# The last group's layer 2 ends and is normalized by pairs of graphs, and all written-out orders of a four-layer graph network are replaced

## The chip, the cores and the metric

The kernel runs on one core of a Trainium2 chip. The metric is device time in microseconds; lower is better. All arithmetic is fp32. TensorE (PE) does the matmuls, VectorE (DVE), ScalarE (ACT) and GpSimd (POOL) do the rest, and SyncE (SP) issues all DMAs in one queue, in order.

## The reference

`x` holds 128 graphs of 128 nodes with 512 features, `adj` a 128 x 128 matrix for each graph. Four layers follow one another; each output is `x = layernorm(x + layer(x, adj))`. Cut to what matters:

```python
# layer 0: GCN, adjacency with self loops, normalized on both sides
An = dh[:, :, None] * (A + I) * dh[:, None, :]          # dh = rsqrt(row sums)
out = relu(einsum('bnm,bmf,fc->bnc', An, X, kernel) + bias)

# layer 1: attention whose weight is one number for a node
q, k = split(X @ W_qk.T);  v = X @ W_v.T                 # 2 x 64 and 512 columns
w = sum((q @ k.T) / 8 * A, axis=-1);  out = softmax(w, axis=nodes) * v

# layer 2: SAGE, own features beside the neighbours' mean
agg = (A @ X) / max(row sums, 1e-6)
out = relu(concat([X, agg]) @ W.T)

# layer 3: GCN again, projection first, without relu
out = L @ (X @ W + b)                                    # L = normalized A + I
```

The norm has no weights: mean and variance over the 512 features of a node, with 1e-5 added to the variance.

## The kernel before

**Groups.** The 128 graphs are taken in 32 groups `t` = 0 to 31 of four graphs, g = 2q + r. Three groups are in flight: while group t runs layer 0 and then layer 1, group t - 1 runs layers 2 and 3. Group 31 is called `last`; its layers 2 and 3 stand alone at the end, with nothing of another group beside them. Groups 0 and 1 have an order of their own (`begin`), since all weights are loaded and prepared there.

**Products.** The 512-wide projections are blocked twofold with seven products in place of eight, B11, T1, T2, B21, B22, T3, T4. Their operands are sums of blocks: of the left side (`agg0s1`, `agg3s2`, `xT1s4`, `inner` and so on, made by POOL or DVE for each group) and of the weights (made once). The four graphs of a group supply the block rows, so `left_sums` needs graphs 2q and 2q + 1 of a pair q. Layer 0 multiplies `agg0` by `wz_sb` into `p_o0`, layer 1 `xT1` by `wv_sb` into `p_v`, layer 2 `xT2` by `wb_sb`, `wa_sb`, `wc_sb` and `wz_sb` in four passes into `p_2x0` to `p_2x3`, layer 3 `agg3` by `wz_sb` into `p_o3`. One 7-piece tile `wz_sb` thus serves layers 0, 2 and 3; for each of them it is filled again piece by piece from copies in DRAM (`w0d`, `w2d`, `w3d`, 256 KB a piece), and a piece can be fetched once the last product on its old contents has run.

**Turning x.** Layers 1 and 2 need `x` transposed. `turn_x` writes it to DRAM (`xT2s`, one transfer for each graph), reads it back block by block (`xT2y`, four reads for each r), and DVE transposes blocks of 32 (`xT2`). In the first groups and the last one, `turn_on_tensor` lets PE do it.

**The end of layer 2.** After the four passes, `y` (the neighbour half) and `v` (the own half, for every node) are complete. For each graph ACT scales its own half into PSUM (`p_2g`), PE adds `arT` times `y` to it, and DVE adds relu of that to `x` and leaves the row sum in a column of `sm`. `norm_last("o2", ...)` then makes the norm for all four graphs at once: the negated mean `nm` (ACT, tile `last1o`), the four sums of squares (ACT, into the single buffer "row"), on POOL the division by 512, the addition of the epsilon (`dme`), the power -1/2 and the product `nmr` (tiles `last3o`, `last4o`), and for each graph a scaling on ACT, or on DVE where it has been moved. `l3_agg` (for the last group `l3_agg_pair`, one pair after another) multiplies the result by the adjacency (`p_agg`), and `l3_out` follows, in the last group by pairs too. The norms of layer 0 and of the last quarter of layer 3 use `bn_stats` instead.

**What sets the order.** Nothing runs in program order. The kernel records every operation with its predecessors (`Plan`), and `schedule` builds each engine's queue from a list of costs. Three written-out tables steer it. `EARLY` shifts the priority of single operations, and `MOVED` names operations that change engine: ACT's copies and scalings go to DVE, two-operand additions change between DVE and POOL. `TIMES` gives for every operation of groups 3 to 29 a due time within a period (`PERIOD` 73637), and within one engine operations with a due time run strictly by it; so the steady groups repeat one order on each of the five queues ("sy", "ve", "gp", "sc", "te"). A key such as `p_o0:3` is the fourth operation on that engine that writes `p_o0` (the product B21), `w0d:2` the third piece fetched (T2). In `MOVED` and `EARLY` the letter in front is the engine, and a letter a, b, c, y or z behind stands for groups 0, 1, 2, 30 or 31. [...] All recorded operations bear line 890 in the profile.

Of the kernel before, what the change touches and what calls it, by code (L numbers as in the profile page):

```python
# [11 lines left out]
FP = mybir.dt.float32  # L12
AF = mybir.ActivationFunctionType
ALU = mybir.AluOpType
AX = mybir.AxisListType

P = 128
K = 32
Q = P // K
G = 4  # L20
F = 512
# [12 lines left out]
    "g:agg0:0": 52, "g:agg0:0b": 110, "g:agg0:0c": -35, "g:agg0:0y": -5, "g:agg0:0z": -425, "g:agg0s1:0": 31,  # L34
    "g:agg0s1:0b": 134, "g:agg0s1:0c": 107, "g:agg0s1:0y": 132, "g:agg0s1:0z": 84, "g:agg0s2:0": 12,
    "g:agg0s2:0b": -210, "g:agg0s2:0c": 123, "g:agg0s2:0y": -361, "g:agg0s2:0z": -261, "g:agg0s4:0": -71,
    "g:agg0s4:0b": -79, "g:agg0s4:0c": 87, "g:agg0s4:0y": 360, "g:agg0s4:0z": 859, "g:agg30:0z": 623,
    "g:agg30s1:0z": 410, "g:agg30s2:0z": 646, "g:agg30s4:0z": 77, "g:agg31:0z": -329, "g:agg31s1:0z": 410,
    "g:agg31s2:0z": 392, "g:agg31s4:0z": 766, "g:agg3:0": 131, "g:agg3:0a": 333, "g:agg3:0b": -88, "g:agg3:0c": -110,
    "g:agg3:0y": -322, "g:agg3s1:0": 75, "g:agg3s1:0a": 528, "g:agg3s1:0b": -174, "g:agg3s1:0c": -73,  # L40
    "g:agg3s1:0y": -982, "g:agg3s2:0": 6, "g:agg3s2:0a": 24, "g:agg3s2:0b": 233, "g:agg3s2:0c": -16,
    "g:agg3s2:0y": 633, "g:agg3s4:0": 130, "g:agg3s4:0a": -4, "g:agg3s4:0b": 225, "g:agg3s4:0c": -489,
    "g:agg3s4:0y": -118, "g:arT:0": -6, "g:arT:0a": 45, "g:arT:0b": -500, "g:arT:0c": -40, "g:arT:0y": -264,
    "g:arT:0z": -170, "g:arT:1": 52, "g:arT:1a": -19, "g:arT:1b": -120, "g:arT:1c": -597, "g:arT:1y": -412,
    "g:arT:1z": 241, "g:d:0": 24, "g:d:0a": 202, "g:d:0b": 597, "g:d:0c": -98, "g:d:0y": 479, "g:d:0z": 577,
    "g:inner:0": 28, "g:inner:0a": -23, "g:inner:0b": 33, "g:inner:0c": -161, "g:inner:0y": -103, "g:inner:0z": -9,
    "g:inner:1": 32, "g:inner:1a": 163, "g:inner:1b": 49, "g:inner:1c": -147, "g:inner:1y": -81, "g:inner:1z": 158,
    "g:inner:2": 62, "g:inner:2a": 14, "g:inner:2b": 333, "g:inner:2c": 228, "g:inner:2y": -362, "g:inner:2z": -769,
    "g:inners1:0": -21, "g:inners1:0a": 207, "g:inners1:0b": 311, "g:inners1:0c": -84, "g:inners1:0y": 211,
    "g:inners1:0z": 1020, "g:inners1:1": 69, "g:inners1:1a": -28, "g:inners1:1b": -19, "g:inners1:1c": 429,  # L50
    "g:inners1:1y": -160, "g:inners1:1z": 52, "g:inners2:0": 6, "g:inners2:0a": 42, "g:inners2:0b": 316,
    "g:inners2:0c": -125, "g:inners2:0y": 934, "g:inners2:0z": 495, "g:inners2:1": 27, "g:inners2:1a": 22,
    "g:inners2:1b": 597, "g:inners2:1c": -319, "g:inners2:1y": 431, "g:inners2:1z": 201, "g:inners4:0": 15,
    "g:inners4:0a": 206, "g:inners4:0b": -185, "g:inners4:0c": 151, "g:inners4:0y": -376, "g:inners4:0z": -365,
    "g:inners4:1": 4, "g:inners4:1a": 46, "g:inners4:1b": 343, "g:inners4:1c": 17, "g:inners4:1y": 855,
    "g:inners4:1z": 35, "g:last3o2_0:0": -2, "g:last3o2_0:0a": -168, "g:last3o2_0:0b": -312, "g:last3o2_0:0c": 71,
    "g:last3o2_0:0y": -1126, "g:last3o2_0:0z": -8300, "g:last3o2_0:1": -5, "g:last3o2_0:1a": -191,
    "g:last3o2_0:1b": 131, "g:last3o2_0:1c": -27, "g:last3o2_0:1y": -274, "g:last3o2_0:1z": -11, "g:last3o2_0:2": -4,
    "g:last3o2_0:2a": -32, "g:last3o2_0:2b": 253, "g:last3o2_0:2c": 125, "g:last3o2_0:2y": 103,
    "g:last3o2_0:2z": -362, "g:last3o3_0:0": 15, "g:last3o3_0:0a": -230, "g:last3o3_0:0b": -70,  # L60
    "g:last3o3_0:0c": -256, "g:last3o3_0:0y": -437, "g:last3o3_0:0z": -808, "g:last3o3_0:1": 22,
    "g:last3o3_0:1a": 380, "g:last3o3_0:1b": -258, "g:last3o3_0:1c": -80, "g:last3o3_0:1y": 1086,
    "g:last3o3_0:1z": 703, "g:last3o3_0:2z": -4121, "g:last3o3_0:3z": 2795, "g:last3o3_1:0z": -1845,
    "g:last3o3_1:1z": 1419, "g:last4o2_0:0": 6, "g:last4o2_0:0a": -46, "g:last4o2_0:0b": -18, "g:last4o2_0:0c": 320,
    "g:last4o2_0:0y": 1210, "g:last4o2_0:0z": 8290, "g:mean_w3:0w": 2, "g:mean_wv:0w": 265, "g:rs:0": -117,
    "g:rs:0a": -100, "g:rs:0b": -43, "g:rs:0c": 86, "g:rs:0y": -127, "g:rs:0z": 357, "g:rstdo0_0:0": 25,
    "g:rstdo0_0:0a": -173, "g:rstdo0_0:0b": 183, "g:rstdo0_0:0c": -144, "g:rstdo0_0:0y": -134, "g:rstdo0_0:0z": -584,
    "g:rstdo0_0:1": 10, "g:rstdo0_0:1a": 160, "g:rstdo0_0:1b": 126, "g:rstdo0_0:1c": 291, "g:rstdo0_0:1y": 1688,
    "g:rstdo0_0:1z": 572, "g:rstdo0_1:0": 36, "g:rstdo0_1:0a": -417, "g:rstdo0_1:0b": 180, "g:rstdo0_1:0c": 120,
    "g:rstdo0_1:0y": -1819, "g:rstdo0_1:0z": -632, "g:rstdo0_1:1": 28, "g:rstdo0_1:1a": 463, "g:rstdo0_1:1b": 20,  # L70
    "g:rstdo0_1:1c": -257, "g:rstdo0_1:1y": 3996, "g:rstdo0_1:1z": 1836, "g:rstdo3_1:0z": -238, "g:rstdo3_1:1z": 2729,
    "g:v1_0:0": 175, "g:v1_0:0a": -3, "g:v1_0:0b": -122, "g:v1_0:0c": 161, "g:v1_0:0y": 536, "g:v1_0:0z": 159,
    "g:v1_0:1": 53, "g:v1_0:1a": -235, "g:v1_0:1b": -130, "g:v1_0:1c": -458, "g:v1_0:1y": -20, "g:v1_0:1z": -54,
    "g:v1_1:0": 2, "g:v1_1:0a": -127, "g:v1_1:0b": -359, "g:v1_1:0c": 283, "g:v1_1:0y": 352, "g:v1_1:0z": 545,
    "g:v1_1:1": -20, "g:v1_1:1a": 3, "g:v1_1:1b": -110, "g:v1_1:1c": 140, "g:v1_1:1y": 268, "g:v1_1:1z": 73,
    "g:v2_0:0": -25, "g:v2_0:0a": -357, "g:v2_0:0b": -330, "g:v2_0:0c": 69, "g:v2_0:0y": -202, "g:v2_0:0z": 138,
    "g:v2_1:0": -30, "g:v2_1:0a": 50, "g:v2_1:0b": 165, "g:v2_1:0c": -151, "g:v2_1:0y": 1510, "g:v2_1:0z": 553,
    "g:w2y1:0w": -79, "g:wa_sb:0w": -55, "g:wb_sb:0w": 48, "g:wb_sb:1w": -280, "g:wb_sb:2w": -90, "g:wb_sb:3w": -170,
    "g:wc_sb:0w": 73, "g:wc_sb:1w": 11, "g:wc_sb:2w": 88, "g:wc_sb:3w": -88, "g:wc_sb:4w": -224, "g:wc_sb:5w": -90,
    "g:xT1:0": -66, "g:xT1:0a": 56, "g:xT1:0b": 74, "g:xT1:0c": -108, "g:xT1:0y": -179, "g:xT1:0z": 469,  # L80
    "g:xT1s1:0": 17, "g:xT1s1:0a": 259, "g:xT1s1:0b": 113, "g:xT1s1:0c": 400, "g:xT1s1:0y": 2729, "g:xT1s1:0z": 1624,
    "g:xT1s2:0": -8, "g:xT1s2:0a": 40, "g:xT1s2:0b": -109, "g:xT1s2:0c": -136, "g:xT1s2:0y": -182, "g:xT1s2:0z": 378,
    "g:xT1s4:0": 19, "g:xT1s4:0a": 169, "g:xT1s4:0b": 19, "g:xT1s4:0c": 3, "g:xT1s4:0y": 257, "g:xT1s4:0z": 172,
    "g:xT2:0": 25, "g:xT2:0a": -1190, "g:xT2:0b": 137, "g:xT2:0c": 150, "g:xT2:0y": -641, "g:xT2:0z": -64,
    "g:xT2:1": 16, "g:xT2:1a": -52, "g:xT2:1b": 897, "g:xT2:1c": 58, "g:xT2:1y": 446, "g:xT2:1z": 651, "g:xT2:2": -34,
    "g:xT2:2a": 54, "g:xT2:2b": -83, "g:xT2:2c": -165, "g:xT2:2y": -342, "g:xT2:2z": 141, "g:xT2s1:0": -35,
    "g:xT2s1:0a": 70, "g:xT2s1:0b": 46, "g:xT2s1:0c": 37, "g:xT2s1:0y": 387, "g:xT2s1:0z": 406, "g:xT2s1:1": 33,
    "g:xT2s1:1a": 218, "g:xT2s1:1b": -344, "g:xT2s1:1c": -47, "g:xT2s1:1y": -1221, "g:xT2s1:1z": -832,
    "g:xT2s2:0": -40, "g:xT2s2:0a": -588, "g:xT2s2:0b": 149, "g:xT2s2:0c": 18, "g:xT2s2:0y": -308, "g:xT2s2:0z": -283,
    "g:xT2s2:1": 47, "g:xT2s2:1a": -167, "g:xT2s2:1b": -30, "g:xT2s2:1c": 52, "g:xT2s2:1y": 1667, "g:xT2s2:1z": 876,  # L90
    "g:xT2s4:0": -25, "g:xT2s4:0a": 166, "g:xT2s4:0b": 536, "g:xT2s4:0c": 103, "g:xT2s4:0y": -764, "g:xT2s4:0z": -38,
    "g:xT2s4:1": 7, "g:xT2s4:1a": -394, "g:xT2s4:1b": -490, "g:xT2s4:1c": 106, "g:xT2s4:1y": -226, "g:xT2s4:1z": 354,
    "s:agg0:0": -59, "s:agg0:0a": -100, "s:agg0:0b": -22, "s:agg0:0c": 4, "s:agg0:0y": 53, "s:agg0:0z": -429,
    "s:agg0:1": 5, "s:agg0:1a": 213, "s:agg0:1b": -168, "s:agg0:1c": -216, "s:agg0:1y": 347, "s:agg0:1z": -324,
# [847 lines left out]
def kernel(  # L942
# [13 lines left out]
    nc = Plan(tc, estimate)  # L956
    B = x.shape[0]
    NT = B // G
    last = NT - 1
# [5 lines left out]
    sp = Pool(nc, ctx.enter_context(tc.tile_pool(name="sp", bufs=3)), 3)  # L965
# [336 lines left out]
    def norm_last(name, t, rows, pairs):  # L1302
# [6 lines left out]
        if name == "o2":  # L1309
            nc.scalar.mul(nm, st["sm", t][:, 2 * rows[0]:2 * rows[0] + n], -1.0 / F)  # L1310
# [514 lines left out]
```

## Time and profile before

| | us |
|---|---|
| runs, median (lowest, highest) | 2421.62 (2421.4, 2425.13) |
| profiled execution, its own time | 2425.63 |
| its span | 2423.8 |
| PE busy in the span | 2358.1 (97%) |
| DVE, ACT, POOL busy | 1759.7 (73%), 1103.7 (46%), 1269.4 (52%) |
| mean granted clock of PE | 0.995 |
| from one `p_ws` to the next, groups 4 to 28, mean and least | 73.28, 72.48 |

Times in the views count from the start of the span. "Idle before" stands in brackets behind a row of the timeline, with what ended it; a row can hold several instructions of one kind (x2), and the time is then that from the first's start to the last's end. `x24` of `p_agg` are three graphs, since an fp32 matmul counts twice and there are four for each graph. DMA-issuing rows on SP ("SPq") show the issue, not the transfer. The view of waits names, for each engine, who came last, with the sum, the number of times and the longest.

### The profile page before, as it was taken

What the parts mean: (1) busy time and instruction counts of PE and PEld (TensorE: products, weight loads), DVE (VectorE), ACT (ScalarE), POOL (GpSimd) and SP (SyncE); (2) the same over time, 40 slices, a digit from 0 to 9 for tenths busy, and PEclk for the clock granted to TensorE, in tenths of its full rate; (3) what the DMA queues carried; (4) which work ended last, traced back from release to release, by engine and by line L of the source; (5) the groups of instructions that cost most, each with busy time, mean ns of one, the idle gap of its engine ahead of it and who ended that gap; (6) DMA issues with size and microseconds to landing.
All of it is one profiled execution on the core that took longest, in us unless ns stands there. A gap on an engine that the chain in (4) does not pass through costs nothing. (4 is left out here: it accounts for less than half of the span.)

```text
span 2423.8 us, 35397 instructions
## 1 busy us (share of the span) xinstructions
PE 2358.1 (97%) x11244; PEld 1938.4 (80%) x11244; DVE 1759.7 (73%) x3611; ACT 1103.7 (46%) x2480; POOL 1269.4 (52%) x1571
## 2 busy tenths in 40 slices
PE   8989999999999999999999999999999999999997
PEld 6767778888878878788878888888888888888776
DVE  5876777677777767777776777777776777777776
ACT  4444444444444445444444444444444444444444
POOL 4345465445565455565455555455654455654434
PEclk9999999999999999999999999999999999999998
DMA  5455575666666665666666756665756675756532
GB/s 148 160 154 162 139 210 167 182 171 183 174 200 166 181 182 170 190 187 172 178 180 174 196 166 182 173 195 168 200 169 180 171 190 169 202 163 189 155 113 79
DMA packets 492106, 417.36 MB, mean 172 GB/s; under 512 B 151824, under 2 KB 375312, under 8 KB 491664
## 3 DMA queue, kind: packets, MB, share of 16 engines
q1 hardware_dynamic: 491920, 415.09, 60.7%
q8 instruction: 91, 1.49, 0.3%
q14 instruction: 95, 0.78, 0.1%
HBM read 297.27 MB, written 117.70 MB: 171 GB/s over the span
## 5 line engine op out<-in xcount | busy, mean ns | idle before, releaser
L890 PE MATMUL p_o<-wz_sb,agg 128*128 128x256 f32 x2048 | 477.5, 380 | 10.0 <-DMA wz_sb<-w0d 3.9
L890 PEld LDWEIGHTS p_o<-wz_sb,agg 128*128 128x128 f32 x2048 | 383.7, 190 | 70.3 <-DMA wz_sb<-w0d 10.9
L890 PE MATMUL p_v<-wv_sb,xT 128*128 128x320 f32 x1024 | 297.1, 433 | 1.3 <-DVE xT L890 1.1
L890 PEld LDWEIGHTS p_agg<-anT,x 128*128 128x128 f32 x2048 | 251.7, 196 | 22.9 <-DVE x L890 8.8
L890 PE MATMUL p_agg<-anT,x 128*128 128x128 f32 x2048 | 257.7, 281 | 9.6 <-DVE x L890 7.0
L890 PEld LDWEIGHTS p_v<-wv_sb,xT 128*128 128x128 f32 x1024 | 191.6, 190 | 87.5 <-DVE xT L890 8.7
L890 ACT COPY agg<-p_agg 128x512 f32<-128x512 f32 (+1 forms) x221 | 116.2, 527 | 252.4 <-PE p_agg L890 251.8
L890 PE MATMUL p_v<-wv_sb,xT1s 128*128 128x320 f32 x768 | 228.1, 433 | 1.5 <-POOL xT1s L890 1.1
L890 PEld LDWEIGHTS p_v<-wv_sb,xT1s 128*128 128x128 f32 x768 | 145.2, 190 | 69.9 <-issue 15.1
L890 PE MATMUL p_o<-wz_sb,agg0s 128*128 128x256 f32 x768 | 183.9, 383 | 11.1 <-DMA wz_sb<-w0d 7.6
L890 DVE TENSOR_TENSOR y<-p_2x,y 128x512 f32<-128x512 f32 (+1 forms) x256 | 158.9, 621 | 38.7 <-PE p_2x L890 34.2
L890 POOL TENSOR_TENSOR y<-u,y 128x1024 f32<-128x1024 f32 (+1 forms) x89 | 178.9, 2010 | 15.0 <-DVE u L890 6.0
L890 PE MATMUL p_o<-wz_sb,agg3s 128*128 128x256 f32 x744 | 176.1, 380 | 1.3 <-POOL agg3s L890 1.3
L890 ACT COPY f_2x<-p_2x 128x512 f32<-128x512 f32 (+1 forms) x122 | 64.7, 531 | 246.4 <-PE p_2x L890 239.8
L890 PEld LDWEIGHTS p_o<-wz_sb,agg0s 128*128 128x128 f32 x768 | 142.6, 190 | 42.8 <-issue 16.9
L890 ACT COPY p_2x<-p_2x 128x512 f32<-128x512 f32 (+1 forms) x216 | 109.1, 516 | 115.5 <-PE p_2x L890 67.6
L890 PEld LDWEIGHTS p_o<-wz_sb,agg3s 128*128 128x128 f32 x744 | 138.9, 190 | 20.2 <-POOL agg3s L890 2.5
L890 POOL TENSOR_TENSOR agg3s<-agg 128x512 f32<-128x512 f32 x29 | 36.7, 1267 | 204.6 <-ACT agg L890 202.2
L890 DVE TENSOR_TENSOR v<-p_v,f_v 128x320 f32<-128x320 f32 x128 | 57.5, 485 | 115.0 <-PE p_v L890 114.8
L890 POOL TENSOR_TENSOR agg<-agg 128x512 f32<-128x512 f32 (+1 forms) x32 | 39.7, 1240 | 190.1 <-DVE x L890 158.6
L890 PE MATMUL p_2g<-y,arT 128*128 128x512 f32 x256 | 121.6, 595 | 2.9 <-DVE y L890 1.8
L890 ACT COPY p_o<-p_o 128x512 f32<-128x512 f32 (+1 forms) x96 | 54.1, 564 | 148.2 <-PE p_o L890 144.4
(233 smaller groups left out, 5322.7 us busy)
## 6 DMA issues: line engine op xcount, KB each, us to landing
wz_sb<-w2d SPq DMA_DIRECT2D x224, 256.0 KB, 3.5
wz_sb<-w3d SPq DMA_DIRECT2D x224, 256.0 KB, 3.8
wz_sb<-w0d SPq DMA_DIRECT2D x203, 256.0 KB, 4.1
x<-in_x_dram SPq DMA_DIRECT2D x31, 1024.0 KB, 5.8
out_dram<-x SPq DMA_DIRECT2D x31, 1024.0 KB, 5.1
xT1s<-x SPq DMA_DIRECT2D x120, 256.0 KB, 2.8
xT1y<-xT1s SPq DMA_DIRECT2D x240, 128.0 KB, 2.7
xT2s<-x SPq DMA_DIRECT2D x120, 256.0 KB, 2.7
```

Of the source, the lines that this page charges most:

```text
L890: op.ins = getattr(getattr(self.nc, op.engine), method)(*[v.real() if isinstance(v, Ref) else v for v in args], **{k: v.real() if isinstan ...
```

## The change

Two things are changed.

1. In `l2_out` of the last group, the loop over the four `p_2g` goes pair by pair (graphs 0, 1, then 2, 3) in place of r by r, and `norm_last` is called after each pair with that pair alone. `norm_last` now takes the columns of the pair out of `sm` and `dme`. For this group there are thus two negated means, two times two squares, and two chains of four POOL operations on two columns, in place of one chain on four. Other groups call it as before.
2. The tables are replaced. In `EARLY` nearly all shifts differ (2226 entries become 2202). In `MOVED` 74 entries go and 57 come. In `TIMES` the same operations get a new order on all five queues; `PERIOD` and the order of the passes stay.

```diff
-            nc.scalar.mul(nm, st["sm", t][:, 2 * rows[0]:2 * rows[0] + n], -1.0 / F)
+            nc.scalar.mul(nm.rearrange("p (r q) -> p r q", r=2),
+                          st["sm", t].rearrange("p (r q) -> p r q", r=2)[:, :, pairs[0]:pairs[-1] + 1], -1.0 / F)
...
             nc.gpsimd.tensor_tensor(rstd.rearrange("p (r q) -> p r q", r=2), rstd.rearrange("p (r q) -> p r q", r=2),
-                                    st["dme", t].rearrange("p (q r) -> p r q", r=2), ALU.add)
+                                    st["dme", t].rearrange("p (q r) -> p r q", r=2)[:, :, pairs[0]:pairs[-1] + 1], ALU.add)
...
         st["sm", t] = sp.tile([P, 4], FP, tag="sm", name=f"smo2_{t}")
-        for r in range(2):
-            for q in range(2):
+        for i in range(2):
+            for j in range(2):
+                r, q = (j, i) if t == last else (i, j)
                 g = 2 * q + r
...
-            norm_stats("o2", t, r, (0, 1))
+            if t == last:
+                norm_last("o2", t, (0, 1), (i,))
+            else:
+                norm_stats("o2", t, i, (0, 1))
```

Of the tables, the entries that the prediction speaks of (steady groups):

```diff
 TIMES, "sy":
-  "xT2y_0:0": 74313, "xT2s_1:0": 74360, "w0d:2": 1056, "xT2y_0:1": 74753
+  "xT2s_1:0": 72660, "w0d:2": 556, "xT2y_0:1": 74253, "xT2y_0:0": 76813
 TIMES, "te":
-  "p_o0:0": 4975, "p_o3:3": 152272, "p_2x0:0": 79264, "p_o0:3": 7384
+  "p_o3:3": 153372, "p_o0:0": 7175, "p_o0:3": 8084, "p_2x0:0": 81764
 MOVED:
-  "s:agg0:0", "s:f_v_0:0", "s:x:9", "s:y1:0", "g:xT1s4:0"
+  "s:agg0:1", "s:p_o0:1", "s:p_v_0:1", "s:v1:1", "s:x:11"
```

A due time of a group's layers 2 and 3 is counted from the group's own start, so `xT2y_0:0` at 74313 falls 676 behind the next group's zero, beside that group's `w0d:2` at 1056. In group 0 the first operation on `ana` (adding the identity) is on DVE now, while the second (the scaling by `d`) stays on POOL; the three of the four sums of layer 0's `wz_sb` that were on POOL are on DVE, where the fourth has been; and two of the four scalings of its layer-2 norm (x:8 and x:10) are on DVE. In the compiled order of the first groups, group 0's first layer-3 `p_agg` comes ahead of group 1's `p_ws`. In the last group `p_2g` keeps its order 0, 2, 1, 3 on PE; the own half of graph 1 is scaled on DVE, and of the four scalings of the norm only that of graph 0 is on DVE (before, that of graphs 0 and 1).

## The prediction

> **What bounds the kernel now.** The page comes first, for the engine that fills the span:
>
> ```profile
> span 2423.8 us, 35397 instructions
> PE 2358.1 (97%) x11244; PEld 1938.4 (80%) x11244; DVE 1759.7 (73%) x3611; ACT 1103.7 (46%) x2480; POOL 1269.4 (52%) x1571
> ```
>
> TensorE is busy for 2358.1 of 2423.8 us. The change adds and removes no matmul, so only the 65.7 us in which PE does nothing (and the half-clock stretches inside the busy time) can be won. The view of time windows places them, cut at the start of group 4's `p_ws` transpose (372.7), of group 28's (2131.43), and at the end of the last `p_2x` product (2387.24; called E below):
>
> ```profile
> 372.70:2131.43 1758.73, 1744.63 (x8355) 1441.56 (x8353) 1282.26 (x2640) 812.53 (x1825) 956.86 (x1176) 1.00 0.64 180
> 2131.43:2387.24 255.81, 249.88 (x1177) 205.08 (x1175) 192.83 (x385) 114.28 (x252) 123.84 (x159) 1.00 0.54 154
> 2387.24:2423.80 36.56, 22.46 (x97) 17.87 (x96) 18.07 (x39) 14.54 (x31) 9.53 (x18) 0.83 0.17 64
> ```
>
> The columns are the stretch, its length, busy PE, weight load, DVE, ACT, POOL, then the clock and the DMA share. PE idles 14.1 us in 24 steady groups, 5.9 in the last groups and 14.1 in the last 36.56 us (of which some 7 lie behind the last product). The head (0 to 372.7) holds the remaining 31. Next the view of PE's waits over the whole span, for the single large ones:
>
> ```profile
> PE p_agg L890 <- DVE x L890: 7.0, 1, 7.0
> PE p_w L890 <- DVE scr L890: 6.1, 1, 6.1
> PE p_a L890 <- POOL ana L890: 3.4, 1, 3.4
> ```
>
> The first is in the tail, the other two in the head. The same view for the steady stretch alone leaves two kinds:
>
> ```profile
> PE p_o L890 <- DMA wz_sb<-w0d: 8.2, 25, 1.0
> PE p_2x L890 <- DVE xT L890: 3.7, 8, 1.0
> ```
>
> The first is a layer-0 product waiting for its piece of `wz_sb`; the second is the first layer-2 product waiting for the transpose of `x`. From one `p_ws` to the next a group takes 73.28 us in the mean and 72.48 at best, so the steady groups together lose about 0.8 us each.
>
> **The steady groups.** One of the slowest (74.92 us from 885.02 on) shows the chain, first on PE and then on SP's queue:
>
> ```profile
> 901.01 0.70 PE L890 MATMUL p_2x<-wb_sb,xT 128*128 128x256 f32 x2 [0.96 <-DVE xT L890]
> 902.10 1.13 PE L890 MATMUL p_o<-wz_sb,agg 128*128 128x256 f32 x4 [0.39 <-DMA wz_sb<-w0d]
> ```
> ```profile
> 892.65 0.32 SPq L890 DMA_DIRECT2D xT2y<-xT2s  x1
> 893.07 0.38 SPq L890 DMA_DIRECT2D xT2s<-x  x1
> 893.55 0.46 SPq L890 DMA_DIRECT2D wz_sb<-w0d  x1
> ```
>
> SP issues in order. At 892.65 it gets past an `xT2y` read that waits until an earlier `xT2s` write has landed; behind it stand the third `xT2s` write and the T2 piece of w0d, both ready before (piece T2's last reader ended some 1.1 us earlier). The new SP order puts those two ahead of that read. The wait itself only moves to the next `xT2y` read, behind which stand three more reads and piece B21, none of them ready sooner. So T2 can go about 1.0 us earlier and the last `xT2s` write about 1.3. On PE the new order swaps layer 3's B21 product with layer 0's B11. Both take 1.73 us: the reader that frees piece B21 ends 1.73 us sooner, and what lies between the fetch and its use grows from 7.3 to 8.6 us. Last, the first `p_2x` product moves behind layer 0's B21 product, 1.73 us later. DVE works against that: two operations (0.70 and about 0.6) now stand before the transpose that it waits for, leaving 0.4, plus the earlier write.
>
> Counting every PE stall above 60 ns in those 24 groups by the product behind it: T1 5.1 us (23 times, its chain unchanged), first `p_2x` 3.7 (8 times, at most 0.96), B21 3.2 (9 times, at most 0.88), T2 1.2. I take 85% of the last three away: 0.85 x 8.1 = 6.9 us, 0.29 per group, and 7.7 us over the 27 groups that follow this order. Bounds: all of them and half of T1's, 10.7 x 27/24 = 12; or nothing.
>
> What the order tightens: layer 2's last product comes 1.73 us sooner after the product before it (4.32 to 2.59, with 1.10 us of slack before on DVE, whose sum now has to be ready about 0.4 us before PE asks); `p_2x` piece 4 of the first pass 1.73 us sooner, slack 0.2 to 1.4; the first `p_2g` 0.9 us sooner behind POOL's 2.36 us `y` addition, slack 0.3. Expected cost 0.06 us per group, 1.7 in all; bounds 0 and 0.8 per group. Four ACT jobs return from DVE (copies of 0.5 to 0.7 us, a scaling of 0.48) and five others of the same sizes go there, one addition returns to POOL (1.27 there, 0.69 on DVE): engines at 73%, 46% and 54% don't bind in sum. Middle: -7.7 + 1.7 = **-6**.
>
> **The head.** The first `ana` addition stood on POOL (7.64, 1.26 us) ahead of the scaling that `p_a` waits for; it goes to DVE behind the `arT` copy (6.74, 0.69), ends at about 8.1, and POOL's scaling (1.04) ends near 9.1 and not 10.01: -0.9. Three of the four `wz_sb` sums move from POOL (1.27 each) to DVE (0.69 each), where `p_o` T2 waits 1.15 us for them; before it, a new order of the four `p_agg` meets a stall of 0.91. Here a rule of the Trainium skill speaks against the move: in "SBUF — State Buffer", section "Terms", VectorE and GpSimd have a shared port pair which one of them holds for a whole instruction while the other stands still. The trace shows it:
>
> ```profile
> 16.82 0.42 DVE L890 TENSOR_TENSOR agg<-agg 128x256 f32<-128x256 f32 x1 [0.84 <-POOL agg0s L890]
> ```
>
> POOL's addition of this size takes 0.73 us at 16.06 and 17.91, but 0.96 at 16.87, beside this row: 0.23 longer. By the rule the three sums on DVE bar POOL for 2.1 us and nothing is won but 3 x 0.58 = 1.7 us of holding; by the row, which is milder, 1.7 plus some overlap. The stalls they can shorten hold only 1.15 + 0.91, so I take -1.3 (bounds 0, if input DMAs, which saturate until 30 us and stand in a new order, become the limit, and -2.1). At 140.4 to 149.4 the hole of 8.1 us is group 0's layer-2 norm: four squares until 145.69, on which the one "row" buffer makes `scr` wait, four POOL operations until 147.77, four scalings on ACT until 150.7. Two of these go to DVE, and the first `p_agg` no longer stands behind `p_ws`: at about 148.1 and not 149.38, -1.3; the 6.1 us wait stays. Head: **-3.5** (bounds -6 and +2).
>
> **The tail.** The chain that ended last:
>
> ```profile
> 2392.76 0.21 ACT last1o L890
> ...
> 2398.38 0.56 DVE x L890
> 2398.94 0.04 issue
> 2398.98 5.48 PE p_agg L890 x24
> 2404.47 0.86 PE p_o L890 x4
> 2405.33 0.89 PE p_agg L890 x8
> ```
>
> Before: the last of four relu-additions ends at E + 5.5; negated mean 0.21, four squares at 0.85, POOL 0.23 + 0.20 + 1.04 + 0.20 with 0.07 between, scaling 0.56: `p_agg` at E + 11.74. After: PE keeps its order 0, 2, 1, 3, so pair 0 waits for the third `p_2g`; the third relu-addition ended at E + 4.6, and the scale of graph 1 on DVE and an earlier last `y1` addition make it 4.3. Then 0.21 + 2 x 0.85 = 6.2; POOL's power on two columns takes 0.70 (layer 1's norm), so 1.33 + 0.3 of gaps = 7.9; scaling 0.56: `p_agg` at **E + 8.5**. Pair 1: ACT is done with its squares at E + 8.1 (a second negated mean, 0.21, and two squares), POOL at E + 9.7, its two scalings on ACT, behind that of graph 1, at E + 11.2. At half clock 24 matmuls of `p_agg` took 5.48, so graphs 0 and 1 fill 8.5 to 12.2 and graph 3 need not wait. `p_o` therefore starts at 14.0 and not 17.2: **-3.2**; the rest runs without a PE gap in both orders. Bounds 0 (pair 1 late by 4) and -6.
>
> Half clock is the second rule. "TensorE: Matmul & The Clock Gate", section "Why this matters for your kernels", asks for no PE gap above some 3 us, else the clock halves. The rows:
>
> ```profile
> 2395.00:2399.00 4.00, 0.02 (x1) 0.02 (x1) 0.62 (x2) 1.94 (x5) 1.67 (x4) 0.50 0.49 180
> 2399.00:2403.00 4.00, 4.00 (x19) 4.00 (x20) 1.85 (x4) 1.09 (x3) 0.00 (x0) 0.50 0.00 0
> ```
>
> The granted clock fell at 2394.09, 2.1 us into a gap of 7.0, and returned at 2404.33, 5.35 us into the work. Full speed (8 in 0.89) would save 5.48 - 2.67 = 2.8 us. The new gap is about 4 us (E + 4.5 to 8.5). By the rule it still halves the clock, gain -3.2; by a gap that falls across two observation windows it doesn't, -6. I take the rule.
>
> **Sum.** -3.5 - 6 - 3.2 = -12.7, and a tenth of that off for waits that appear behind shortened ones: about **-12**. Made on the profiled execution (2425.63 us: span 2423.8 and 1.8 around it), it would come to 2413.6. That execution is 4.0 above the median of the runs, 2421.62, from which I count: **2409.6**.
>
> **Rivals.** (a) *The ends alone move.* The pieces of w0d share 16 DMA engines that are 64% busy; if their landing times and not SP's order set the stalls, the middle stays: 2421.62 - 6 = 2415.6. For it: the T1 stall, 23 times, has no queue in front of it. Against: the `xT2s` write and T2 visibly stand behind a waiting read. (b) *A new stall per group*, the one with the other sign: layer 2's last product, or the first `p_2g`, asks before DVE or POOL has its sum. Each 0.1 us costs 2.7 us over 27 groups; from 0.45 us on the whole gain of 12 is gone, from 0.63 the kernel is measurably slower; 0.7 gives 2428. For it: slacks of 0.2 to 0.4 us on three products. Against: each lies beside slack of the same size. (c) *The pairs bring nothing*: graph 3's scaling ends so late that PE waits again, 12 - 3 = 9: 2412.6.
>
> **How the numbers follow.** The forecast has 0.50, (a) 0.20, (b) 0.15, (c) 0.15. About 0.2%, 4.8 us, is what a measurement of this kernel tells from no change. The forecast and (c) are nearly all faster, (a) at -6 a little more than half, (b) mostly slower: faster 0.70, same 0.17, slower 0.13. The forecast's own range is 2403 to 2416; with (a), (c) and most of (b), and the lower bounds of head, middle and tail together about -20, it is 2401 to 2426.
>
> **What would show it.** Mean group 73.05 us and no more than 1.5 us of waits `p_2x <- xT` and of B21 together; T1's stall as before. First tail `p_agg` at E + 8.5, and its p_agg x24 still near 5.5. First `p_a` wait near 2.5; the `p_w` wait unchanged. Waits of `p_2x` or `p_2g` for DVE `u` or POOL `y` in every group would make it wrong, as would a middle that keeps 14 us of idle PE.

## The result and the profile after

The changed kernel takes 2399.26 us (median of 4, 2395.63 to 2404.17) against 2422.74 before (2421.4 to 2425.13): ratio 0.9903, 95% interval 0.9883 to 0.9923, so 23.5 us less. The forecast was 12 less, 2409.6, with a range from 2401. The direction and the mechanism in the steady groups held; the size did not. Two later measurements, on chips 13 and 5, gave 0.9920 (0.9907 to 0.9933), 18.4 us, and 0.9915 (0.9902 to 0.9929), 21.0 us.

The page of the changed kernel, in the lines that answer to those of before:

```profile
span 2402.4 us, 35529 instructions
PE 2351.9 (98%) x11244; PEld 1945.0 (81%) x11244; DVE 1763.4 (73%) x3614; ACT 1100.9 (46%) x2464; POOL 1289.2 (54%) x1589
```

The span shrank by 21.4 us. The profiled execution took 2404.17 us, the longest of the four, so this is on the low side of the gain. PE's busy time fell too, by 6.2 us, with the same 11244 matmuls; the part on why the size failed comes back to this. The time windows, cut at the same events as before (group 4's `p_ws`, group 28's, the end of the last `p_2x`):

```profile
372.64:2117.08 1744.44, 1737.31 (x8354) 1445.65 (x8353) 1289.94 (x2641) 804.13 (x1801) 984.38 (x1200) 1.00 0.64 181
2117.08:2370.02 252.94, 250.31 (x1178) 205.66 (x1177) 190.31 (x380) 118.15 (x260) 125.44 (x158) 1.00 0.54 155
2370.02:2402.36 32.34, 21.23 (x96) 16.68 (x95) 17.79 (x40) 14.14 (x31) 9.15 (x20) 0.90 0.20 73
```

By stage: head 372.70 to 372.64, nothing; 24 steady groups 1758.73 to 1744.44, 14.3; last groups 2.9; from E to the end 4.2. SP's queue in one steady group, whose `p_ws` starts at 881.44, shows the new order:

```profile
884.65 1.62 SPq L886 DMA_DIRECT2D xT2s<-x  x3
887.21 0.33 SPq L886 DMA_DIRECT2D wz_sb<-w0d  x1
887.64 2.30 SPq L886 DMA_DIRECT2D xT2y<-xT2s  x5
```

The last `xT2s` write and piece T2 now stand ahead of all reads. T2's piece leaves 5.8 us behind `p_ws`, where it left at 8.5 in the group at 885.02 that the prediction shows (medians of 25 groups: 5.83 and 6.97). PE's waits in the steady stretch, and three single ones over the whole span:

```profile
PE p_o L886 <- DMA wz_sb<-w0d: 6.2, 7, 1.4
```
```profile
PE p_w L886 <- DVE scr L886: 5.1, 1, 5.1
PE p_agg L886 <- DVE x L886: 4.1, 1, 4.1
...
PE p_a L886 <- POOL ana L886: 2.7, 1, 2.7
```

In the steady groups the wait of `p_2x` for the transpose is gone. Of the 6.2 us of waits for w0d, 4.8 are T1's piece (five times) and 1.3 are B21's (twice, 0.70 and 0.64). None of the products whose distance the change tightened waits there. The chain of the tail starts PE at E + 8.5 (2370.02 to 2378.50):

```profile
2374.54 0.82 ACT squareo L886 x2
2375.39 0.81 ACT squareo L886 x2
...
2377.67 0.21 POOL last4o L886
2377.90 0.56 DVE x L886
2378.50 4.57 PE p_agg L886 x24
2383.08 0.86 PE p_o L886 x4
2383.94 0.89 PE p_agg L886 x8
```

Two squares stand ahead of the first `p_agg` now, not four. The granted clock was half from 2379.08 to 2382.49 only, 3.41 us, and the 24 matmuls took 4.57.

### The profile page after: what moved, and what is told of

Read it like the earlier page. It is cut to its first block, busy times and chain, and to the rows that moved or that the text cites. A ratio compares the mean times of both kernels' runs of the same rounds, so it can differ in the third digit from the quotient of the medians.

```text
span 2402.4 us, 35529 instructions
## 1 busy us (share of the span) xinstructions
PE 2351.9 (98%) x11244; PEld 1945.0 (81%) x11244; DVE 1763.4 (73%) x3614; ACT 1100.9 (46%) x2464; POOL 1289.2 (54%) x1589
## 4 chain that ended last, share of the span: by engine, by line
PE 90%; DMA 4%; DVE 2%; POOL 1%; SPq 1%; ACT 1%; issue 1%; POOLq 0%; DVEq 0%; ACTq 0%
PE p_o L886 29%; PE p_2x L886 27%; PE p_v L886 19%; PE p_agg L886 9%; PE p_2g L886 4%; DMA wz_sb<-w0d 3%; PE p_sc L886 1%; SPq L886 1%; DVE x L886 1%; DVE y L886 0%; DMA w3d<-wc_sb 0%; DMA w0d<-wz_sb 0%; PE p_warm L886 0%; DMA xT2s<-x 0%; ACT squareo L886 0%
## 5 line engine op out<-in xcount | busy, mean ns | idle before, releaser
L886 POOL TENSOR_TENSOR agg0s<-agg 128x512 f32<-128x512 f32 (+1 forms) x30 | 37.2, 1241 | 191.0 <-DVE x L886 170.8
L886 POOL TENSOR_TENSOR xT<-xT 128x512 f32<-128x512 f32 (+1 forms) x91 | 98.0, 1077 | 72.6 <-DVE dh L886 56.5
L886 ACT ACTIVATE squareo<-x 128x512 f32<-128x512 f32 x127 | 79.9, 629 | 78.3 <-DVE x L886 78.2
```

What stands on the lines that cost most here:

```text
L886: op.ins = getattr(getattr(self.nc, op.engine), method)(*[v.real() if isinstance(v, Ref) else v for v in args], **{k: v.real() if isinstan ...
```

## The experiments

All times are medians; "before" is the kernel before, measured beside each run on the same chip. The tables of the two kernels can be mixed by keys: those without a group letter belong to the steady groups.

### The steady tables alone

```diff
 kernel before
-TIMES, and EARLY and MOVED for keys without a group letter: of before
+TIMES, and EARLY and MOVED for keys without a group letter: of the changed kernel
```

> The kernel before with the new entries for the steady groups alone: all of TIMES, and of EARLY and MOVED the keys without a letter for a first or last group. Head, tail and the code are those of before. Theory now (a stall costs the time from one product's start to the next one's, not the idle time the trace shows): the first p_2x product, T2's and B21's piece and what hangs on them cost 14.4 us in 24 groups, so 2422 - 16 = 2406, mean group 72.7, head and tail as before. By the prediction's own sizing (only idle time counts): -7, 2415. By its rival (DMA landing times set the stalls): no change, 2422.

Measured: 2430.97 against 2415.79, ratio 1.0057 (1.0044 to 1.0070): 15 us slower, which no theory had. The 24 steady groups did as expected, 1743.0 us or 72.63 each. The loss lies at the joins, where the order of the first groups passes into the steady one and that into the order of the last groups. Group 4's `p_ws` came at 387.5, and the stretch from group 28 to E took 266.1 (255.8 before). So this run says nothing on the total; only its steady stage can be read.

### The ends alone

```diff
 changed kernel
-TIMES, and EARLY and MOVED for keys without a group letter: of the changed kernel
+TIMES, and EARLY and MOVED for keys without a group letter: of before
```

> The changed kernel with the steady groups' tables of before; the code and the tables of the first and last groups are the new ones. Theory now: the tail gives 4.2, the last groups about 1, the head nothing: 2417. The prediction: head -3.5 and tail -3.2: 2415. If the head's tables cost time once the steady groups are the old ones: 2420 or more.

Measured: 2421.76 against 2415.79, ratio 1.0022 (1.0012 to 1.0031), slower. The join is broken here as well: 266.8 us from group 28 to E. The other stages can be read: group 4's `p_ws` at 371.8, E to the first `p_agg` 8.47, and 72.92 us for a group of the old steady order.

### The pairs alone

```diff
 changed kernel
-EARLY, MOVED, TIMES: of the changed kernel
+EARLY, MOVED, TIMES: of before
```

> The changed code (pairs in the last group) with all tables of before; only some 50 matmuls at the very end stand in another order. Theory: the pairs themselves bring the first p_agg from E + 11.7 to about E + 8.5 and the time to 2422 - 3 = 2419. Rival (the gain comes from the tail's new order and not from the pairs): within 1 us of before.

Measured: 2415.78 against 2415.79, ratio 0.9998 (0.9989 to 1.0007): no change. The first `p_agg` came at E + 11.0. POOL's timeline of this run shows why:

```profile
2387.55 0.24 POOL L2921 TENSOR_SCALAR last3o<-last2o 128x2 f32<-128x2 f32 x1 [6.87 <-ACT squareo L2921]
2387.87 0.19 POOL L2921 TENSOR_TENSOR last3o<-last3o,dme 128x2 f32<-128x2 f32 x1
2388.40 0.22 POOL L2921 TENSOR_SCALAR last3o<-last2o 128x2 f32<-128x2 f32 x1 [0.33 <-ACT squareo L2921]
```

The first two are pair 1's; pair 0 begins at 2388.40, since by the old priorities ACT took pair 0's second square as the last of the four. Splitting a chain brings nothing until the order puts one half first.

### The head's old tables in the changed kernel

```diff
 changed kernel
-EARLY and MOVED for the weights and groups 0, 1, 2: of the changed kernel
+EARLY and MOVED for the weights and groups 0, 1, 2: of before
```

> The changed kernel with the head's tables of before (keys of groups 0, 1, 2 and of the weights). Theory now, from the two traces (group 4's p_ws at 372.7 and 372.6): the head's new tables bring nothing, 2399 +- 1. The prediction: they bring 3.5, so this one is at 2403. If the half-clock stretches of the new head (20.5 us against 13.7) are its own doing: below 2399.

Measured: 2417.31 against 2415.79, ratio 1.0006 (0.9997 to 1.0015). Against the changed kernel's gain of 18 to 23 us in its three measurements, the old head costs nearly all of it. Group 4's `p_ws` fell at 384.7, 12.0 us later than in the first profile of the changed kernel, and this wait is most of it (1.1 us in the profile of before, none in that of after):

```profile
PE p_v L2920 <- POOL xT1s L2920: 8.9, 1, 8.9
```

POOL runs `xT1s` of group 3, the first steady one, only behind the four norm operations of group 2 (278.03 to 279.95), which wait for ACT's squares; in the changed kernel `xT1s` comes 11.5 us ahead of them. This is the price of the join and not the worth of the head. The mixed runs show that the tables of head, middle and tail were made for one another.

### The changed kernel again

> The changed kernel once more, beside the following runs. In the runs so far the steady order of before took 72.87 and 72.92 us per group (kernel with pairs alone, kernel with the new ends alone) and 73.28 in the profile of before; the new one 72.58 to 72.69 in all. Theory: the gain depends on how late DMA pieces land in an execution: steady -7 to -14, last groups and tail -7: -14 to -21 against before of the same call. If the 23 us of the first measurement are a fixed gain: -23.

Measured: 2397.02 against 2415.39, ratio 0.9920 (0.9907 to 0.9933), 18.4 us. Group 4's `p_ws` came at 366.25 here, not at 372.64 as in the first profile.

### SP's order alone

```diff
 kernel before, TIMES
-"sy": of before
+"sy": of the changed kernel
```

> The kernel before with SP's new steady order alone; TensorE's order is the old one, exactly. Theory: piece T2 and the xT2 reads leave about 1 us earlier, so T2's stall (1.8 us in 24 groups) and most of that of the first p_2x product (4) go, B21's stays: -3 to -6. Rival (landing times and not SP's order set the stalls): within 1 us of before.

Measured: 2408.4 against 2415.39, ratio 0.9969 (0.9959 to 0.9979): -7.0, with the queues of TensorE and ScalarE exactly the old ones. From group 5 to group 25 SP's queue alone differs; at the two joins the compiled order of POOL and DVE shifts with it. The steady stretch, and PE's only wait in it:

```profile
373.63:2117.70 1744.07, 1737.77 (x8354) 1444.37 (x8353) 1282.60 (x2640) 811.79 (x1825) 960.88 (x1176) 1.00 0.63 181
```
```profile
PE p_o L2921 <- DMA wz_sb<-w0d: 5.0, 8, 1.3
```

That is 72.67 us for a group. B21's stall went too, which the expectation denied: the `xT2y` reads ahead of B21's piece wait for the last `xT2s` write to land, and that write leaves 2.2 us sooner now (4.23 us behind `p_ws` in the median, 6.42 in a profile of before on chip 5). B21's piece itself leaves 0.5 us sooner than there and lands 1.0 sooner (13.73 against 14.72). SP's new order also changes the order of the reads among themselves and of two `w2d` pieces; what each of these moves is worth was not run by itself.

### One swap on TensorE alone

```diff
 kernel before, TIMES "te"
-"p_2x0:0": 79264, "p_o0:3": 7384
+"p_2x0:0": 81764, "p_o0:3": 8084
```

> The kernel before with one change on TensorE in the steady groups: the first p_2x product stands behind layer 0's B21 product; SP's queue is the old one. Theory: the wait of p_2x for the transpose goes (3 to 4 us), but the B21 product asks for its piece 0.43 us sooner and waits more: 0 to -3. Rival (this swap alone carries the steady gain): -7 or more.

Measured: 2423.67 against 2415.39, ratio 1.0037 (1.0023 to 1.0051): +8.3, where 0 to -3 was expected. PE's waits in its steady stretch:

```profile
PE p_o L2921 <- DMA wz_sb<-w0d: 14.5, 19, 1.9
PE p_o L2921 <- DVE xT L2921: 2.6, 2, 1.7
```

The wait for the transpose had covered one for B21's piece behind it. Taking the first away moves the second product 0.43 us forward, into a piece that lands at 15.05 us behind `p_ws` in the median, while the product asks at about 14.3 (T2's starts at 12.55 and takes 1.73).

### T1's product later

```diff
 changed kernel, TIMES "te"
-"p_o0:1": 3845      (ahead of layer 3's T2 product)
+"p_o0:1": 3974      (behind it)
```

> The changed kernel with one more swap in the steady groups: layer 0's T1 product stands behind layer 3's T2 product, 1.73 us later. T1's piece is the one stall that the change leaves: 5.5 us in 24 groups of the profile of after, 13 times, and the product that waits runs 0.10 longer. Theory: all of it goes, 5 to 8 us faster than the changed kernel. Rival: what hangs on T1's result (the copy f_o, T3) comes late instead: no gain over the changed kernel, or a loss.

Measured: 2459.98 against 2415.39, ratio 1.0184 (1.0168 to 1.0200): 45 slower than before, 63 slower than the changed kernel. The waits over its span name what stands behind it:

```profile
PE p_o L2880 <- POOL agg3s L2880: 41.9, 26, 1.6
PE p_o L2880 <- ACT p_o L2880: 22.8, 26, 1.2
```

Layer 3's T2 product needs a sum that POOL ends just in time for its old place, and layer 0's T1 product was what covered it. T1's stall can't be cured by this swap.

### Before and after on one chip

> The kernel before, profiled on the chip of the next three runs, so that stages can be compared on one chip. Time as before. Theory (the cost of the steady stalls depends on how late DMA pieces land): its 24 steady groups take 1747 to 1751 us if this chip is like the one of the pairs-alone run, 1759 if like that of the first profile; group 4's p_ws at 372 to 375, by where the half-clock stretch of the start falls.

> The changed kernel on that chip. Against the profile of before there: up to group 3's p_ws -3, 24 steady groups -5 to -14 (1742 to 1745), from group 28 to E -3, from E to the last product -4. In all -15 to -23.

Measured: 2415.48 against 2416.74 (ratio 0.9999), and 2395.76 against 2416.74, ratio 0.9915 (0.9902 to 0.9929). The windows, head to tail, of before and of the changed kernel:

```profile
0.00:372.56 372.56, 341.36 (x1622) 273.88 (x1623) 266.74 (x547) 162.71 (x373) 179.20 (x219) 0.98 0.55 159
372.56:2119.94 1747.38, 1740.97 (x8355) 1442.86 (x8354) 1283.67 (x2640) 813.57 (x1825) 963.29 (x1176) 1.00 0.63 181
2119.94:2373.89 253.95, 250.14 (x1177) 204.68 (x1175) 192.87 (x385) 114.50 (x252) 124.60 (x159) 1.00 0.54 155
2373.89:2410.18 36.29, 22.23 (x96) 17.66 (x96) 18.08 (x39) 14.55 (x31) 9.53 (x18) 0.87 0.17 63
```
```profile
0.00:367.18 367.18, 338.60 (x1622) 274.52 (x1623) 265.43 (x554) 164.68 (x373) 170.17 (x211) 0.99 0.56 162
367.18:2107.85 1740.67, 1736.43 (x8355) 1445.66 (x8354) 1290.85 (x2641) 804.81 (x1801) 984.37 (x1200) 1.00 0.63 182
2107.85:2359.96 252.11, 249.73 (x1178) 205.85 (x1177) 190.45 (x380) 118.08 (x260) 125.40 (x158) 1.00 0.54 156
2359.96:2393.40 33.44, 22.33 (x96) 17.71 (x95) 17.78 (x40) 14.13 (x31) 9.15 (x20) 0.87 0.20 71
```

This is the "last chip" (chip 5) below. Here head 5.4, steady groups 6.7, last groups 1.8, tail 2.9, in all 16.8. The profiled execution of before, 2412.05, was 3.4 us below the median of its runs, which is most of what is missing to 21.0.

### The tail alone

```diff
 kernel before, with the pairs
-EARLY and MOVED of group 31 behind the p_2x products: of before
+EARLY and MOVED of group 31 behind the p_2x products: of the changed kernel
```

> The kernel before with the pairs and, for the work after the last p_2x products alone, the new entries of EARLY and MOVED (the last 28 matmul groups stand otherwise). Theory: pair 0's two squares and its POOL chain now come first, where the pairs-alone run had them behind pair 1's: first p_agg at E + 8.5 and not 11.0, last product at E + 26.2 and not 29.9: 3.5 to 4 faster than before. Rival (what the tail gains is lost in the half clock): E + 8.5, but the last product at E + 28 or later, under 2.

Measured: 2416.9 against 2416.74, ratio 1.0003 (0.9994 to 1.0012): nothing. That is the rival's time, but neither its start nor the theory's came out. PE's timeline:

```profile
2387.87 3.78 PE L2928 MATMUL p_agg<-anT,x 128*128 128x128 f32 x16 [4.11 <-DVE x L2928]
2392.67 3.78 PE L2928 MATMUL p_agg<-anT,x 128*128 128x128 f32 x16 [1.03 <-ACT x L2928]
```

The start came at E + 9.6. Then graph 2 stood third on PE and not graph 3 as in the changed kernel, and PE waited 1.03 us for its scaling; half clock lasted 10.24 us (2386.34 to 2396.58), through all four graphs. The last product ended at E + 30.4, as before (30.0 to 30.2). So the run did not rebuild the changed kernel's tail, and says only that pairs with this order bring nothing.

### SP's order and the swap

```diff
 kernel before, TIMES
-"sy": of before;   "te" "p_2x0:0": 79264, "p_o0:3": 7384
+"sy": of the changed kernel;   "te" "p_2x0:0": 81764, "p_o0:3": 8084
```

> The kernel before with SP's new steady order and, on TensorE, the first p_2x product behind layer 0's B21 product. SP's order alone gave -7.0, this swap alone +8.3. Theory (the swap costs because B21's piece is late behind SP's waiting read; once SP's order is mended it lands in time): within 1.5 us of SP's order alone, so -6 to -8. Rival (the swap costs by itself): about +1.

Measured: 2409.18 against 2416.74, ratio 0.9971 (0.9961 to 0.9981): -7.6, the same within the intervals as SP's order alone on chip 13 (-7.0). The swap that cost 8.3 by itself costs nothing once the piece is in time.

## Why the prediction was right or wrong

**Steady groups: mechanism right, the size is the term that failed.** SP's order is what mattered: alone it brought 7.0 us, and its steady groups took 72.67 us where those of the changed kernel took 72.60 on the same chip. It has the T2 and `xT2s` transfers ahead of the waiting read as the prediction named. The prediction gave B21's relief to the swap on PE, though, and the write 1.3 us where it gained 2.2. What failed is the step "Counting every PE stall above 60 ns in those 24 groups by the product behind it": it took the idle time between records for the cost of a stall, 8.1 us for the three that were to go, of which 6.9 were to be won. The stage gave 14.3. In the rows of the windows PE's idle time fell from 14.1 to 7.1 us, close to the forecast 6.9; the other 7.3 came off the time recorded as busy (1744.63 to 1737.31), for the same matmuls. The idle time of PE's records leaves out part of each stall. From the profile before, a `p_2x` pair in a group with a stall and in one without:

```profile
607.57 0.70 PE L890 MATMUL p_2x<-wb_sb,xT 128*128 128x256 f32 x2 [0.52 <-DVE xT L890]
1706.45 0.59 PE L890 MATMUL p_2x<-wb_sb,xT 128*128 128x256 f32 x2
```

Matmul records are 0.38 us long but start 0.22 apart, so a wait of up to 0.16 behind one hides under its modelled end. And the matmul that has waited is 0.48 long: the pair is 0.10 longer. A stall thus costs what is shown plus 0.26, and one below 0.16 shows no idle at all. Times from the start of one product to the start of the next, summed in us over the 24 groups, have no such hole. In the changed order and with the swap, B21 and not `p_2x` follows T2, so B21's wait for its piece stands in the first row there:

| from the start of | before, first profile | after, first profile | before, last chip | after, last chip | SP's order alone | swap alone |
|---|---|---|---|---|---|---|
| layer 0's T2 (before, next is `p_2x`, which waits for `xT`) | 47.20 | 43.12 | 43.06 | 41.48 | 41.44 | 57.28 |
| first `p_2x` (before, next is B21, which waits for its piece) | 17.08 | 10.36 | 12.38 | 10.36 | 10.49 | 10.36 |
| layer 3's T3 (next waits for T2's piece) | 43.27 | 41.44 | 41.44 | 41.44 | 41.44 | 41.57 |
| layer 0's B21 | 43.08 | 41.66 | 42.50 | 41.60 | 41.55 | 42.87 |
| layer 3's T2 (next is layer 0's B11 before) | 41.89 | 41.44 | 43.43 | 41.44 | 43.55 | 42.50 |
| layer 3's B11 and layer 0's T1 | 93.79 | 95.09 | 92.35 | 93.01 | 93.36 | 94.74 |

A product without a stall takes 41.44 in this count, a `p_2x` 10.36. By the first four rows, the three stalls held 16.0 us in the first profile of before, where I read 8.1; 1.9 of it stayed (B21's wait in two groups), and 14.1 went. The rest nearly cancels, and the stage's 14.3 are found. The share that I let go, 85%, was about right; the 1.7 us for new waits was not, since no run of the changed kernel showed any. T1's chain stayed, as forecast, and even cost 1.3 more in that execution.

**And the size is not fixed.** On the last chip the same order of before lost only 6.7 against the new one, close to the 5.3 that the prediction had for 24 groups; the three stalls held 4.7 us there. What the forecast lacks on that chip is spread over the stages: head 5.4 for 3.5, steady groups 6.7 for 5.3, last groups 1.8 for 0.7, against tail 2.9 for 3.2. These four are read from the windows; no run shows the gain of head, last groups or tail by itself, since the mixed sets lose at their joins. B21's piece landed at 15.04 us behind `p_ws` in the median of the first profile and at 14.72 on the last chip, with the product asking at 14.8. Three tenths of a microsecond around that point, 24 times, come to 7 us, the size of the difference. Rival (a), by which landing times and not SP's order set the stalls, is refuted by SP's order alone. That landing times set how much the old order loses fits these two profiles, but no run varied them, and why the pieces landed later in the first is open.

**The swap of layer 3's B21 and layer 0's B11** was counted for B21's piece. SP's order alone cured B21. What the swap can have done is on B11: its stall (43.43 to 41.44, 2.0 us on the last chip; 0.5 in the first profile) went in the changed kernel and stayed with SP's order alone. This is read from the traces; that swap was not run by itself.

**Rival (b), a new stall per group,** did not come in the changed kernel. The run with T1's product moved shows how near it lay: 1.73 us at one place cost 63 us.

**Head: forecast -3.5; 0 in the first profile, -5.4 on the last chip.** Two more profiles with these tables have group 4's `p_ws` at 366.25 and 366.72, so the first one is the exception. The parts are mixed. `p_a` waited 2.7 and not 3.4 (forecast 2.5). `p_w`'s hole fell by 1.0, though it was to stay. The `wz_sb` sums on DVE brought nothing there: `p_o` T2 still waits 1.2 us for them, so the -1.3 was wrong. In both pairs of profiles 2.7 and 3.2 us are won between group 3's `p_ws` and group 4's, under no step of the forecast. The difference between the two profiles of the changed kernel goes with half clock. On the last chip both kernels had 3.41 us of it at the start, then 10.24 (before) and 6.83 (after) around group 0's norm. The first profile of the changed kernel had 6.83 at the start, 6.83 at the norm and two stretches of 3.41 more, at 98.98 and 269.64. At half speed 10.2 us of matmuls lose 5.1, which is the size of the difference (372.64 against 367.18). The second of these two stretches began behind this gap, which stands in the last chip's profile as well (second row) and halved no clock there:

```profile
269.56 1.96 PE L886 MATMUL p_2g<-y,arT 128*128 128x512 f32 x2 [1.66 <-ACT p_2g L886]
```
```profile
265.59 1.95 PE L886 MATMUL p_2g<-y,arT 128*128 128x512 f32 x4 [1.66 <-ACT p_2g L886]
```

So a gap of 1.66 us, well under the 3 of the prediction's rule, can halve the clock in one execution and not in another. In each of the fourteen profiles all changes of the clock inside the run lie whole multiples of 3.41 us apart, but at another offset from the kernel's start in each; that where a gap falls on this grid decides is argued from these rows and was not tried.

**Tail: forecast -3.2; measured -4.2 and -2.9.** The start of `p_agg` at E + 8.5 came to within 0.02 us on both chips. The gate rule, taken by the prediction, held in that the gap of 4.1 us did halve the clock each time; but for 3.41 us in two profiles of the changed kernel (24 `p_agg` in 4.57) and for 6.83 in that on the last chip (5.49). These 0.9 us are most of the difference between the two tails. In the kernel before, the pairs brought nothing, neither alone nor with the tail's new entries, so rival (c) lay nearer than its 0.15. That the order pays only if pair 1 is as punctual as in the changed kernel is read from the two timelines.

**Last groups** were given 0.7 us by the sum and gave 1.8 to 2.9; several small waits go (1.3 for `xT2s` and 1.1 for `xT`, among others), which I had listed under no step.

**The range** ended at 2401, from low ends that came to -20 together. With 14.0 in place of 8.1 for 24 groups, 15.8 for 27, the forecast's own sum, without the 1.7 and the tenth off, would have been -22.5, or 2399. That this meets the measured 2399.26 is in part luck: the head that it counts with 3.5 gave 0 in that profile, and last groups and tail gave more.

## What to carry to other kernels

Size a TensorE stall from the start of one product to the start of the next, against the same pair in a group that doesn't stall, and not by the idle time of the records. In a queue that issues in order, look for what stands ready behind a waiting transfer: SP's new order, with two such transfers moved to the front, was worth 7 us here, while a swap on the engine that seemed to wait cost 8, because one wait covered another. Tables that fix an order can't be judged in parts: a mixed set shows its joins, and only stages away from the joins may be compared.

## What was not expected of the hardware

The kernel before took 73.28 us per group in its first profile and 72.81 in that on the last chip, with B21's piece, 256 KB, landing 0.3 us earlier there and T2's 0.2. Three runs with the old steady order gave 72.87 to 72.92; five with the new one gave 72.53 to 72.69. The medians of the kernel before spread over 7.3 us in four measurements (2415.39 to 2422.74), those of the changed kernel over 3.5 in three (2395.76 to 2399.26). So the order with slack seems less sensitive as well as faster, but this rests on the first measurement alone.

Half-clock stretches inside the runs came in whole steps of 3.41 us, and the same gap of 4.1 us in the tail cost one step in three profiles, two in three others and, in the run of the tail alone, three.
